# Local attention on one core: weighted values laid out by features, softmax weights divided before their transposes, q's unit length inside the exponential

## The chip, the cores and the metric

The kernel runs on one core of a Trainium2 chip. The metric is the device time of one execution in microseconds. Before the change three executions took 3894.79, 3896.19 and 3896.57 us; their median is 3896.19 us. The profile is of a further execution, which took 3893.85 us; the span of its instructions is 3892.1 us.

## The reference

The input is 8 sequences of 512 tokens with 128 features, in float32. Two blocks follow each other, each with a layer norm ahead, a layer norm behind and a residual. The first is a causal attention with a Taylor-expanded exponential. The second, which the change concerns, is a stack of six layers. Each has local attention with 16 heads of 64 features and windows of 32 tokens, and a gated feed-forward part:

```python
q = l2norm(q) * qs;  k = l2norm(k) * ksc            # unit length, then a scale by feature
q = q * cos * scale + rotate_half(q) * sin * scale  # rotary; k with 1 / scale
# a window of 32 queries sees its own 32 keys and the 32 before: bk2, bv2
sim = jnp.einsum('bhwie,bhwje->bhwij', bq, bk2) * 8.0
mask = (it < jb) | (it > jb + w) | (jb == -1)
sim = jnp.where(mask, -max, sim)
attn = jax.nn.softmax(sim, -1)
out = jnp.einsum('bhwij,bhwje->bhwie', attn, bv2)
x = x + out.reshape(b, n, INNER) @ Wo
# then x = x + (a * gelu(gate)) @ W2 + b2 of a layer norm of x
```

The length of q is one number for a token and a head. Since the rotation is linear, this number may be multiplied in before or after it, or into the scores.

## The kernel before

**Stages.** The first block is done in the first 535 us of the span. The rest is one loop over steps t. A unit is a block of 128 tokens of one sequence in one layer: 6 layers x 8 sequences x 4 blocks are 192 units. Each step begins one unit and goes on with the units begun up to six steps earlier, so that a step holds projections of unit t, scores of unit t-1, weighted values of unit t-2 and the output projection of unit t-3. After the fourth block of a sequence the feed-forward part follows in pieces, one piece a step: the norm with its four transposes (`feed_norm`), `feed_first` (transposes of the normed tokens), `feed_middle` (the hidden products and gelu), `feed_last`. So four steps make a cycle, each with another piece in it.

**What a step computes.** `proj` multiplies the tokens with the weights of q (s = 0) or k (s = 1) on PE (L421). DVE multiplies the result by the rotary tables (`turned` L429, `straight` L436), ACT squares it (L444), DVE adds the squares up (L457), POOL adds the two rotary parts (L454). `unit_length` turns the sums of squares into inverse lengths on ACT, and POOL multiplies q and k by them (L470). `by_features(c)` transposes q and k of four head pairs on PE (by the helper of L70), and ACT copies them out of PSUM (L514). `values` makes the values (L481), which ACT copies (L482) and seven DMAs on SP's queue spread over windows. `scores` writes a mask into PSUM by a product with a 128x128 unit matrix in BF16 (L527), twice, for even and odd heads; adds the products of q and k, 64 of them of 64x32 stationary and 64 moving columns (L534); takes the row maxima on DVE (L542), 16 exponentials on ACT, one a head (L546), and the sums and their reciprocals on DVE (L552, L553). `by_keys` transposes the unnormed weights (L564 copies). `weigh_values` multiplies with the weights as stationary operand (64x32) and the values as moving operand (64 columns) (L574), giving tokens by features; DVE divides by the sums (L582). `out_by_features` transposes the result (L70, copies L596), and `out_project` multiplies by Wo (L603) and adds into the state (L608).

**Order.** On PE the order is the order of the program text, fixed by hand. On the other engines a scheduler decides, with copies out of PSUM raised in priority and with a few hand-written orders (`issue_behind`). The order on PE within a step, with the unit's lag behind, is: `proj` q (0), `out_project` (3), `proj` k (0), `by_keys` (2), `values` (0), `by_features(0)` (1), `weigh_values` (2), `by_features(4)` (1), the feed-forward piece, `scores` (1), `out_by_features` (2).

**Buffers in PSUM.** The tag mm has two buffers of two banks (projections, values, hidden products), tr has two of one bank (all transposes and the output projection), and s has one of two banks, which scores and weighted values use in turn. Buffers are given out in the order of the program.

A float32 product is two passes on PE, each with its own weight load, so 64 products are 128 records of each kind.

## Time and profile before

| what | before |
|---|---|
| median of three runs | 3896.19 us |
| the profiled execution | 3893.85 us, span 3892.1 us |
| PE busy | 3729.8 us (96%), 65600 products and as many weight loads |
| DVE busy | 2818.2 us (72%) |
| ACT busy | 2657.5 us (68%) |
| POOL busy | 1837.0 us (47%) |
| mean busy share of the DMA engines, 535 to 3810 us | 26% |
| granted TensorE clock | 0.99 |

A name such as `tr<-ident,qk` means that the instruction writes the tile tr and reads ident and qk. L70 is the line of a helper that all transposes share, so transposes are told apart by their tiles. Busy PE is not PE at its peak, since products are pipelined and their ends are modelled; where the pace of PE matters, the distance between starts is used.

### The profile page before, as it was taken

What the parts mean: (1) busy time and instruction counts of PE and PEld (TensorE: products, weight loads), DVE (VectorE), ACT (ScalarE), POOL (GpSimd) and SP (SyncE); (2) the same over time, 40 slices, a digit from 0 to 9 for tenths busy, and PEclk for the clock granted to TensorE, in tenths of its full rate; (3) what the DMA queues carried; (4) which work ended last, traced back from release to release, by engine and by line L of the source; (5) the groups of instructions that cost most, each with busy time, mean ns of one, the idle gap of its engine ahead of it and who ended that gap; (6) DMA issues with size and microseconds to landing.
All of it is one profiled execution on the core that took longest, in us unless ns stands there. A gap on an engine that the chain in (4) does not pass through costs nothing.

```text
span 3892.1 us, 149565 instructions
## 1 busy us (share of the span) xinstructions
PE 3729.8 (96%) x65600; PEld 2474.2 (64%) x65600; DVE 2818.2 (72%) x4300; ACT 2657.5 (68%) x6745; POOL 1837.0 (47%) x1311
## 2 busy tenths in 40 slices
PE   8999989999999999999999999999999999999997
PEld 4555456666666666666666666666666666666665
DVE  4555567777867777777777777777787777777775
ACT  5565656776767777777777677777677777766664
POOL 0000025555555555555555555555555555555552
PEclk9999999999999999999999999999999999999998
DMA  2000012222222222222222322223222222222221
GB/s 81 17 9 12 6 50 71 59 66 60 76 74 63 63 63 66 71 75 65 60 62 64 82 65 66 65 56 82 70 66 59 66 65 56 65 68 68 64 67 37
DMA packets 153208, 233.46 MB, mean 60 GB/s; under 512 B 32622, under 2 KB 53356, under 8 KB 151788
## 3 DMA queue, kind: packets, MB, share of 16 engines
q1 hardware_dynamic: 152556, 223.89, 22.4%
q8 instruction: 517, 8.47, 0.9%
q14 instruction: 135, 1.11, 0.1%
HBM read 24.54 MB, written 4.19 MB: 7 GB/s over the span
## 4 chain that ended last, share of the span: by engine, by line
PE 89%; ACT 5%; issue 3%; DVE 2%; DMA 0%; POOL 0%; POOLq 0%; DVEq 0%; SPq 0%; ACTq 0%
PE tr L70 17%; PE mm L421 17%; PE mm L481 9%; PE py L603 9%; PE sp L534 7%; PE po L574 6%; PE y L282 4%; PE mm L625 3%; PE py L657 3%; PE mm L626 3%; PE sc L252 2%; PE sp L527 2%; ACT sq L444 2%; PE vv L230 2%; PE po L318 2%
## 5 line engine op out<-in xcount | busy, mean ns | idle before, releaser
L454 POOL TENSOR_TENSOR qk<-t,t 128x1024 f32<-128x1024 f32 x384 | 909.2, 2368 | 999.6 <-DVE t L436 999.5
L421 PE MATMUL mm<-wqkv,state 128*128 128x512 f32 x1536 | 727.1, 596 | 3.7 <-ACT v L482 2.6
L470 POOL TENSOR_TENSOR qk<-qk,ss 128x1024 f32<-128x1024 f32 x384 | 722.3, 1902 | 16.0
L429 DVE TENSOR_TENSOR t<-mm,tab 128x512 f32<-128x512 f32 x768 | 497.8, 685 | 242.8 <-PE mm L421 231.3
L546 ACT ACTIVATE pe<-sp,mx 128x64 f32<-128x64 f32 x3072 | 651.4, 376 | 27.6 <-DVE mx L542 27.3
L436 DVE TENSOR_TENSOR t<-mm,tab 128x1024 f32<-128x1024 f32 x384 | 465.9, 1213 | 0.0
L457 DVE TENSOR_REDUCE ss<-sq 128x16 f32<-128x1024 f32 x384 | 461.9, 1203 | 2.0 <-ACT sq L444 2.0
L444 ACT ACTIVATE sq<-mm 128x512 f32<-128x512 f32 x768 | 422.6, 610 | 47.2 <-DVE t L436 45.6
L603 PEld LDWEIGHTS py<-oT,wo 128*128 128x128 f32 x3072 | 374.8, 193 | 93.5 <-issue 56.2
L70 PEld LDWEIGHTS tr<-ident,qk 128*128 128x128 f32 x3072 | 345.7, 141 | 127.1 <-issue 105.7
L70 PE MATMUL tr<-ident,qk 128*128 128x128 f32 x3072 | 412.1, 277 | 7.4 <-ACT qT L514 2.3
L596 ACT COPY oT<-tr 128x512 f32<-128x512 f32 x384 | 207.3, 589 | 266.2 <-PE tr L70 265.2
L421 PEld LDWEIGHTS mm<-wqkv,state 128*128 128x128 f32 x1536 | 264.1, 192 | 191.6 <-issue 188.0
L481 PE MATMUL mm<-wqkv,state 128*128 128x512 f32 x768 | 367.9, 602 | 16.8 <-ACT sq L444 16.8
L603 PE MATMUL py<-oT,wo 128*128 128x128 f32 x3072 | 376.0, 276 | 1.0 <-ACT oT L596 0.9
L582 DVE TENSOR_TENSOR on<-po,su 128x1024 f32<-128x1024 f32 x192 | 235.1, 1224 | 170.1 <-PE po L574 170.1
L534 PEld LDWEIGHTS sp<-kT,qT 64*32 64x32 f32 x24576 | 271.9, 106 | 116.7 <-issue 113.8
L574 PE MATMUL po<-v,pT 64*32 64x64 f32 x24576 | 299.3, 225 | 44.7 <-issue 44.7
L482 ACT COPY v<-mm 128x1024 f32<-128x1024 f32 x192 | 194.5, 1013 | 211.0 <-PE mm L481 211.0
L534 PE MATMUL sp<-kT,qT 64*32 64x64 f32 x24576 | 312.2, 227 | 26.0 <-issue 25.2
L574 PEld LDWEIGHTS po<-v,pT 64*32 64x32 f32 x24576 | 258.5, 105 | 86.4 <-issue 86.2
L542 DVE TENSOR_REDUCE mx<-sp 128x16 f32<-128x1024 f32 x192 | 234.6, 1222 | 106.9 <-PE sp L534 106.3
(108 smaller groups left out, 5171.0 us busy)
## 6 DMA issues: line engine op xcount, KB each, us to landing
v<-v SPq DMA_DIRECT2D x1152, 128.0 KB
v<-v SPq DMA_DIRECT2D x672, 64.0 KB
wqkv<-in_L_ffn_Wqkv_dram SPq DMA_DIRECT2D x6, 1536.0 KB
wo<-in_L_ffn_Wo_dram SPq DMA_DIRECT2D x6, 512.0 KB
xin<-_attn_hidden_states_dram SPq DMA_DIRECT2D x8, 256.0 KB
xr<-_attn_hidden_states_dram SPq DMA_DIRECT2D x8, 256.0 KB
x<-xr SPq DMA_DIRECT2D x8, 256.0 KB
xr<-x SPq DMA_DIRECT2D x8, 256.0 KB
```

Of the source, the lines that this page charges most:

```text
L70: nc.tensor.transpose(ps[:cols, :rows], src, ident[:rows, :rows])
L421: nc.tensor.matmul(ps[:, a].rearrange("p h d -> p (h d)"), lhs, wqkv[:, s, a, :], start=True, stop=True)
L429: nc.vector.tensor_tensor(t2[:, a], ps[:, 1 - a], tab[:, 2 * s + 1, j, HF * a : HF * (a + 1)].unsqueeze(1).to_broadcast([P, H, HF]), ALU.mult,
L436: nc.vector.tensor_tensor(t1, ps, tab[:, 2 * s, j, :].rearrange("p (a d) -> p a d", a=2).unsqueeze(2) .to_broadcast([P, 2, H, HF]), ALU.mult,)
L444: nc.scalar.activation(sq[:, :, a, :], ps[:, a], AF.Square)
L454: nc.gpsimd.tensor_tensor(qk[:, s].rearrange("p h a d -> p a h d"), t1, t2, ALU.add)
L470: nc.gpsimd.tensor_tensor(t, t, ss[:, i, :].unsqueeze(2).to_broadcast([P, H, HD]), ALU.mult)
L481: nc.tensor.matmul(ps[:, p, :], lhs, L["wqkv"][:, 2, p, :], start=True, stop=True)
L534: nc.tensor.matmul(sp[W * w : W * (w + 1), p, pair, :], qT[HD * p : HD * (p + 1), pair, W * w : W * (w + 1)], kT[HD * p : HD * (p + 1), pa ...
L546: ex = nc.scalar.activation(pe[:, pair, p, :], sp[:, p, pair, :], AF.Exp, bias=mx[:, p, pair : pair + 1])
L574: nc.tensor.matmul(po[W * w : W * (w + 1), p, pair, :], pT[r, pair, W * w : W * (w + 1)], v2[r, w, HD * pair : HD * (pair + 1)], start=Tru ...
L603: nc.tensor.matmul(py, L["wo"][:, c, :], oT[:, c, :], start=(c == 0), stop=(c == NP - 1))
```

## The change

Eight edits come together.

1. `weigh_values` swaps operands: the values are stationary (64x64) and the weights move (32 columns), so that the result comes out by features. ACT copies it in one piece of 128x1024. `out_by_features` is gone, and Wo's rows are reordered on the host to fit.
2. The division by the sums moves ahead of `by_keys`: two halves, each a sum and a reciprocal on DVE and a product on POOL.
3. q is no longer multiplied by its inverse length on POOL. The 16 exponentials take it as a scale by token, and one small product on DVE applies it to the row maxima.
4. The mask product has 32 rows and a 32x128 stationary matrix (`each`), even and odd heads on different rows; the first block of a sequence keeps the 128-row form.
5. The copy of the values is split: half on ACT, half on DVE, with `values` in two halves.
6. The order on PE becomes `proj` q, `out_project`, `proj` k, `by_features(0)`, first half of `values`, `by_keys`, second half of `values`, `weigh_values`, `by_features(4)`, the feed-forward piece, `scores`.
7. New orders by hand: squares of q behind the exponentials, copies of `by_features` behind the squares of q, the rotary products of k (`turned`) behind the reciprocals, POOL's additions behind the divisions.
8. The gelu table is loaded behind the copies of `by_keys`, no longer ahead of the step.

```diff
+    each = const.tile([2 * W, P], BF16, tag="each", name="each")
...
     def gelu_only():
         ld = nc.scalar.preload_act_table_set("gelu_and_others")
-        issue_behind(ld, exps[-1])
+        issue_behind(ld, pcopies[-1])
...
-            nc.vector.tensor_tensor(
+            t = nc.vector.tensor_tensor(
                 t2[:, a], ps[:, 1 - a],
...
+            if s == 1 and sums:
+                issue_behind(t, sums[-1])
...
+            q2 = nc.scalar.activation(sq[:, :, a, :], ps[:, a], AF.Square)
+            if s == 0:
+                if exps:
+                    issue_behind(q2, exps[-1])
+                qsquares.append(q2)
...
+        add = nc.gpsimd.tensor_tensor(qk[:, s].rearrange("p h a d -> p a h d"), t1, t2, ALU.add)
+        if divisions:
+            issue_behind(add, divisions[-1])
...
-        for i in range(2):
-            t = qk[:, i].rearrange("p h a d -> p h (a d)")
...
+        t = qk[:, 1].rearrange("p h a d -> p h (a d)")
+        nc.gpsimd.tensor_tensor(t, t, ss[:, 1, :].unsqueeze(2).to_broadcast([P, H, HD]), ALU.mult)
...
+        nc.tensor.matmul(ps[:, half, :], lhs, L["wqkv"][:, 2, half, :], start=True, stop=True)
+        if half == 0:
+            nc.scalar.copy(v0[:, 0], ps[:, 0])
+            return
+        nc.vector.tensor_copy(v0[:, 1], ps[:, 1])
...
-                nc.scalar.copy(dst, ps)
+                cp = nc.scalar.copy(dst, ps)
+            issue_behind(cp, qsquares[-1])
...
         for p in range(2):
+            r = slice(W * p, W * (p + 1))
+            lhs, mk = (identb, mask0) if u["j"] == 0 else (each[r], mask[r])
             nc.tensor.matmul(
-                sp[:, p], identb, mk.unsqueeze(1).to_broadcast([P, NP, 2 * W]),
+                sp[:, p], lhs, mk.unsqueeze(1).to_broadcast([lhs.shape[0], NP, 2 * W]),
...
+        rn = u["ss"][:, 0, :].rearrange("t (c p) -> t c p", p=2)
...
             nc.vector.tensor_reduce(mx, sp, AX.X, ALU.max, negate=True)
+            nc.vector.tensor_tensor(mx, mx, rn.rearrange("t c p -> t p c"), ALU.mult)
...
-                    pe[:, pair, p, :], sp[:, p, pair, :], AF.Exp, bias=mx[:, p, pair : pair + 1]
+                    pe[:, pair, p, :], sp[:, p, pair, :], AF.Exp,
+                    bias=mx[:, p, pair : pair + 1], scale=rn[:, pair, p : p + 1],
...
-        su = f2.tile([P, NP, 2], F32, tag="su", name="su")
-        nc.vector.tensor_reduce(su, pe, AX.X, ALU.add)
-        nc.vector.reciprocal(su, su)
+        for c in range(0, NP, 4):
+            part = pe[:, c : c + 4].rearrange("t c p k -> t (c p) k")
+            su = f2.tile([P, NP], F32, tag=f"su{c}", name="su")
+            with tc.high_priority():
+                nc.vector.tensor_reduce(su, part, AX.X, ALU.add)
+                rc = nc.vector.reciprocal(su, su)
+                dv = nc.gpsimd.tensor_tensor(
+                    part, part, su.unsqueeze(2).to_broadcast([P, NP, 2 * W]), ALU.mult
+                )
...
-        po = psum.tile([P, 2, NP, HD], F32, tag="s", name="po", bufs=1)
...
+        po = psum.tile([P, 2, NP // 2, P], F32, tag="s", name="po", bufs=1)
+        for k in range(NP // 2):
             for w in range(4):
+                for i in range(2):
+                    for p in range(2):
+                        r, c, o = slice(HD * p, HD * (p + 1)), 2 * k + i, HD * (i ^ p)
+                        nc.tensor.matmul(
+                            po[o : o + HD, p, k, W * w : W * (w + 1)],
+                            v2[r, w, HD * c : HD * (c + 1)],
+                            pT[r, c, W * w : W * (w + 1)],
+                            start=True, stop=True, skip_group_check=True,
+                        )
+        u["oT"] = oT = f1.tile([P, 2, NP // 2, P], F32, tag="oT", name="oT")
         with tc.high_priority():
-            dv = nc.vector.tensor_tensor(
...
+            nc.scalar.copy(oT, po)
...
-            if gelus:
-                gelu_only()
             at(t, 0, proj, 0)
             at(t, 3, out_project)
             at(t, 0, proj, 1)
-            at(t, 2, by_keys)
...
-            at(t, 0, values)
...
+            at(t, 1, by_features, 0)
+            at(t, 0, values, 0)
+            at(t, 2, by_keys)
+            if gelus:
+                gelu_only()
+            at(t, 0, values, 1)
...
-            at(t, 1, by_features, 0)
             at(t, 2, weigh_values)
...
             at(t, 1, scores)
-            at(t, 2, out_by_features)
```

## The prediction

> **What bounds the kernel now.** I first read busy shares and the chain that ended last on the page.
>
> ```profile
> span 3892.1 us, 149565 instructions
> ...
> PE 3729.8 (96%) x65600; PEld 2474.2 (64%) x65600; DVE 2818.2 (72%) x4300; ACT 2657.5 (68%) x6745; POOL 1837.0 (47%) x1311
> ...
> PE 89%; ACT 5%; issue 3%; DVE 2%; DMA 0%; POOL 0%; POOLq 0%; DVEq 0%; SPq 0%; ACTq 0%
> ```
>
> PE is the bound, with ACT and DVE in 7% of the chain. The timeline of PE for one step (start, length, instructions) says where:
>
> ```profile
> 2067.54 1.88 PE L421 MATMUL mm<-wqkv,state 128*128 128x512 f32 x4
> 2069.26 1.95 PE L603 MATMUL py<-oT,wo 128*128 128x128 f32 x16
> 2071.05 1.88 PE L421 MATMUL mm<-wqkv,state 128*128 128x512 f32 x4
> 2072.76 1.04 PE L70 MATMUL tr<-ident,pe 128*128 128x128 f32 x8
> 2073.64 1.88 PE L481 MATMUL mm<-wqkv,state 128*128 128x512 f32 x4
> 2075.36 1.04 PE L70 MATMUL tr<-ident,qk 128*128 128x128 f32 x8
> 2076.32 1.49 PE L574 MATMUL po<-v,pT 64*32 64x64 f32 x128
> 2077.74 1.09 PE L70 MATMUL tr<-ident,qk 128*128 128x128 f32 x8
> 2078.67 0.60 PE L70 MATMUL nx<-ident,state 128*128 128x128 f32 x4
> 2079.12 0.59 PE L527 MATMUL sp<-mask,identb 128*128 128x512 bf16 x2
> 2079.65 1.61 PE L534 MATMUL sp<-kT,qT 64*32 64x64 f32 x128
> 2081.19 1.09 PE L70 MATMUL tr<-ident,on 128*128 128x128 f32 x8
> 2082.12 1.88 PE L421 MATMUL mm<-wqkv,state 128*128 128x512 f32 x4
> ```
>
> One piece starts where the last ends: 14.58 us without a wait. From the starts of q's projection between 665 and 3258 us, the four kinds of step take on average 20.2 (hidden products), 17.0 (last products), 15.1 (norm) and 15.9 (transposed norm): 68.2 us a cycle, 48 cycles. The norm lengthens DVE's work, so the step after it is late (15.9 for a like amount of PE work).
>
> What the other engines do in this step:
>
> ```profile
> 2068.26 3.39 ACT L546 ACTIVATE pe<-sp,mx 128x64 f32<-128x64 f32 x16
> ...
> 2072.04 1.09 ACT L444 ACTIVATE sq<-mm 128x512 f32<-128x512 f32 x2 [0.39 <-DVE t L436]
> ...
> 2077.84 1.23 DVE L582 TENSOR_TENSOR on<-po,su 128x1024 f32<-128x1024 f32 x1 [0.41 <-PE po L574]
> ```
>
> The exponentials follow each other every 0.196 us ((3.39 - 0.45)/15) and end 4.1 us after the step's start; their transposes run at 5.2. That slack of 1.1 us is what the change draws on.
>
> **The skill.** "ScalarE: Activation LUTs", What ACT_TABLE_LOAD costs: each operand read by a [128,1] pointer adds about 93 ns to an activation. The trace agrees for one pointer: groups by shape have `ln_rs<-ln_mv,eps` (4 elements, pointer bias) at 297 ns but `ss<-ss` (32 elements, none) at 230, and gelu on 128x512 (pointer) at 687 against 610 for the square. No run here shows two pointers. "TensorE: Matmul & The Clock Gate", LDWEIGHTS: a load takes its columns / 1.2 ns, whatever its rows. The timeline agrees: `vs<-cb,tw`, 128 weight columns and 4 moving, starts 16 times between 15.47 and 17.35 us, 0.117 each. "TensorEngine Tiling (Array Packing)", Key Properties: tiles load and multiply independently. Eight passes of L282 (128x64 weights, 512 moving) start at 27.82 and the next piece at 29.69: 1.87, where L421 needs 1.72 for four, so two column tiles do run side by side.
>
> **What PE gains, by part.**
>
> - `out_by_features` goes: 0.93 us (2081.19 to 2082.12).
> - Mask: two products over 0.53. On different rows they can run together: minus half of the 0.43 that the chain gives them, 0.21, in three steps of four: 0.16.
> - Weighted values: now 1.42 from start to start. Each pass will load 64 columns and move 32, so loads set the pace: half of 0.117, 0.058 on a tile; four tiles side by side make 0.0147 a pass, times 128 is 1.88. I take 1.85: +0.43. Lower end 0 (if issue alone sets the pace, as the old 1.42/128 = 0.011 could be); upper end, two loads on the same rows not side by side, 128 x 0.029 = 3.7: +2.3.
>
> Sum -0.66 a step, 127 us in 192: what the change brings if PE stays the bound.
>
> **What the other engines lose.** ACT per step: two copies of oT (2 x 0.48 paced) become one of about 1.0 (as L482, 1013 ns); half of L482 leaves (-0.5); the scale pointer adds 0.085 (mean of the trace's 0.077 and the skill's 0.093) to each of 16 exponentials: +1.36. DVE: minus 1.22 (L582), plus 0.65 for half the values (L234: 687 ns), 0.25 for the product on the maxima (like L553: 243 ns), 0.25 for a second reciprocal and 0.1 for splitting the sum: even. POOL: minus 1.9 (L470), plus two products of 128x512 at 1.04 (the additions of 512 and 1024 elements in L677 and L454 give 2.15 ns an element; 1902 less 512 x 1.67 for the broadcast form): even. Eight copies for `each` (under 1 us once) and the DMAs, whose number stays, lie beside other work.
>
> No engine is full, but the chain around the softmax grows at both ends. Before, `out_by_features` gave the maxima 0.93 us of cover, so the exponentials began 0.72 after the step's start. Now scores are PE's last work: maxima 0.2 to 1.4, product to 1.65, exponentials from 1.7. A walk through a step, in us after its start, in the order in which each engine has its instructions:
>
> - ACT: exponentials issued to 1.7 + 16 x 0.281 = 6.2, done 6.3; squares of q (0.49 each) to 7.2, the first done at 6.8; copies qT, kT to 8.15, done 8.3.
> - DVE: second sum 6.4 to 7.05, reciprocal 7.3; POOL's second division 7.4 to 8.45.
> - PE, free at 6.1 after `by_features(0)`: first half of `values` waits for the square, 6.85 to 7.7; `by_keys` waits for the copy of qT, 7.95, and for the second division, 8.6 to 9.0; second half of `values` to 9.9; weighted values to 11.75; `by_features(4)` to 12.6. Without waits this would be 11.2: 1.4 lost.
> - DVE after the reciprocal: `turned`, sum of squares, `turned`, `straight` of k to 10.95. ACT: squares of k to 12.0, oT to 12.95, then qT and kT of the second half to 14.0. The mask needs the buffer of the weighted values, so it waits for oT; the second half of the scores waits for kT.
>
> Then mask 0.31 and scores 1.5. Hidden products (2042.94 to 2048.17: 5.23) cover oT: 12.6 + 5.23 + 1.81 = 19.65; last products (2.58): 17.0; to both 0.15 for the gaps called issue, which now stand at 0.3 and which waits partly fill. Norm step: mask at 13.05, kT at 14.0, end 14.9, call it 15.0. Step after it: DVE's norm now precedes the maxima whole, and ACT's squares of k come 0.7 later, so exponentials start 3.2 after the step's start (before: 1.66 in the step from 2082.12). Everything shifts by 1.5: squares of k end 13.5, oT 14.5, qT 15.0; the norm's transposes take the PSUM buffer that this copy frees: 15.0 to 15.6; mask and scores to 17.4. The old mask once a cycle adds 0.2. Sum 19.8 + 17.15 + 15.0 + 17.4 + 0.2 = 69.55, against 68.2: +1.35 a cycle, x48 = +65 us. On the profiled execution (span 3892.1, time 3893.85) that is 3957 and 3959; on the median, 2.3 us above it, 3961.
>
> Queued behind the new waits: on POOL the divisions hold back the additions (2.37 each, L454), but with these, the copy of kT and the product on k (1.9) POOL is done near 17 us, ahead of k's transposes in the next step (5.6 us into it). On SP the DMAs of the second half of the values wait for DVE's copy, which ends at 11.65; the products that read them come a whole step later, so they stay hidden. The gelu table moves behind pT: 9.7 to 11.0, where ACT waits for `straight`, so it costs nothing; if DVE were earlier, it would cost up to its 1.28 in one step of four.
>
> **Rivals.**
>
> *PE gain comes through (faster).* The scale pointer is free, or bias and scale are read together. Then exponentials end 1.36 earlier; the path through the first reciprocals and the divisions holds back 0.9 of this on the two PE-heavy steps, so each gains about 0.45; norm step -0.45, the step after -0.8: 67.4 a cycle, -38 us, 3858. With weighted values at the old pace also, 65.8: 3781. For it: PE 96% busy, 1.1 us of slack. Against: one pointer costs its time in this trace. It decides near a pace of 0.23 us for an exponential.
>
> *Weight loads on the same rows don't overlap.* Weighted values 3.7, all on PE's path: +1.85 more a step, 3961 + 355 = 4316. For it: no 64x64 tile in this trace. Against: today's 64x32 loads, 27 ns by the skill's price, start every 0.011, closer than two row halves alone would allow (0.0135).
>
> *Gain and loss cancel.* The walk leans on waits of a few tenths; within 0.2% (8 us, about what a measurement here can tell from no change) is a narrow slot.
>
> **Numbers.** Slower through the longer softmax chain 0.54; loads not overlapping 0.07; PE gain through 0.34; cancel 0.05. So slower 0.61, same 0.05, faster 0.34. Likeliest time 3961; its own range, from 0.2 us less to 0.3 more a step, 3915 to 4025. The range over all leaves out half of the rival with old pace and the loads: 3810 to 4040.
>
> **What would show it.** Right: exponentials every 0.28 us; PE waiting before `values` on squares and before `by_keys` on POOL or ACT, 1 to 1.5 us a step; weighted values 1.8 from start to start; no L70 on `on`; the step after the norm over 17 us. Wrong: exponentials still every 0.2 us, PE without waits, weighted values near 1.4 or 3.7.

## The result, and the profile after

The changed kernel took 4364.5 us (4356.4 to 4366.3) where the kernel before took 3895.5 (3892.3 to 3896.6): the ratio is 1.120, with a 95% interval of 1.118 to 1.122. The forecast was 3961 us. The side was right; of the 469 us that it became slower, 65 were foreseen.

The page of the changed kernel, the busy shares and the chain that ended last:

```profile
PE 3832.1 (88%) x64064; PEld 2472.2 (57%) x64064; DVE 2905.0 (67%) x4884; ACT 2834.1 (65%) x6558; POOL 1879.6 (43%) x1503
...
PE 57%; ACT 25%; DVE 12%; issue 5%; ACTq 0%; POOL 0%; DMA 0%; DVEq 0%; POOLq 0%; SPq 0%
ACT pe L567 18%; PE mm L493 10%; PE tr L77 9%; PE po L606 9%; PE sp L552 5%; DVE mx L562 5%; ACT sq L454 4%; PE y L289 3%; PE mm L643 3%; PE py L675 3%; PE mm L644 3%; DVE mx L563 2%; PE sc L259 2%; PE mm L428 2%; PE vv L237 1%
```

PE's share of the chain fell from 89% to 57%, and the exponentials (L567) alone hold 18%. PE alone is no longer the bound: the chain now runs through the softmax on ACT and DVE, and PE waits for it inside nearly every step. Here is PE's timeline of a norm step of the changed kernel (start, length, instructions), the counterpart of the step that the prediction showed:

```profile
2260.33 1.98 PE L428 MATMUL mm<-wqkv,state 128*128 128x512 f32 x4
2262.15 1.95 PE L621 MATMUL py<-oT,wo 128*128 128x128 f32 x16
2263.93 1.88 PE L428 MATMUL mm<-wqkv,state 128*128 128x512 f32 x4
2265.65 1.07 PE L77 MATMUL tr<-ident,qk 128*128 128x128 f32 x8
2268.06 1.12 PE L493 MATMUL mm<-wqkv,state 128*128 128x512 f32 x2 [1.33 <-ACT sq L454]
2269.02 1.04 PE L77 MATMUL tr<-ident,pe 128*128 128x128 f32 x8
2269.89 1.09 PE L493 MATMUL mm<-wqkv,state 128*128 128x512 f32 x2
2270.91 2.07 PE L606 MATMUL po<-pT,v 64*64 64x32 f32 x128
2272.91 1.09 PE L77 MATMUL tr<-ident,qk 128*128 128x128 f32 x8
2273.84 0.60 PE L77 MATMUL nx<-ident,state 128*128 128x128 f32 x4
2274.38 0.39 PE L545 MATMUL sp<-mask,each 32*128 32x512 bf16 x2
2274.69 1.71 PE L552 MATMUL sp<-kT,qT 64*32 64x64 f32 x128
2276.33 1.98 PE L428 MATMUL mm<-wqkv,state 128*128 128x512 f32 x4
```

It lasts 16.0 us against 14.58. The transposes of `on` (0.93) are gone and the mask takes 0.31, as announced; weighted values take 2.00 from start to start instead of 1.42, and 1.33 us are a wait of `values` for the squares of q. ACT in the same step shows what those squares stand behind:

```profile
2262.18 4.85 ACT L567 ACTIVATE pe<-sp,mx,ss 128x64 f32<-128x64 f32 x16 [4.87 <-DVE mx L563]
2266.82 1.18 ACT L454 ACTIVATE sq<-mm 128x512 f32<-128x512 f32 x2
```

Sixteen exponentials follow each other every 0.29 us ((4.85 - 0.49)/15 = 0.291; the median distance of two starts in the whole run is 0.290), where it was 0.196. The list of waits of the changed kernel (engine, waiting piece, releaser; us in total, times, longest), from which two of the six longest are shown, says that PE's wait for the squares is the rule: the weight load of `values` has it in 189 of 192 steps, with 1.65 us each (312.0 over 189).

```profile
ACT pe L567 <- DVE mx L563: 648.0, 189, 5.5
...
PEld mm L493 <- ACT sq L454: 312.0, 189, 4.1
```

By kinds of step, as the prediction counted them (average distances between the starts of q's projection in the middle of the run, in us; the forecast of a cycle holds 0.2 more for the old mask):

| | hidden products | last products | norm | after the norm | cycle |
|---|---|---|---|---|---|
| before | 20.2 | 17.0 | 15.1 | 15.9 | 68.2 |
| forecast | 19.8 | 17.15 | 15.0 | 17.4 | 69.55 |
| after | 21.1 | 21.4 | 16.6 | 18.8 | 77.9 |

48 times the 8.36 us that the cycle is longer than forecast are 401 us, nearly all that was missed. Half of it is in one kind, the step with the last products. There the small product on the row maxima does something that it does in no other step; the timelines of VectorE and POOL:

```profile
2239.15 1.23 DVE L562 TENSOR_REDUCE mx<-sp 128x16 f32<-128x1024 f32 x1 [0.27 <-PE sp L552]
2240.48 1.88 DVE L563 TENSOR_TENSOR mx<-mx,ss 128x16 f32<-128x16 f32 x1
...
2261.91 0.17 DVE L563 TENSOR_TENSOR mx<-mx,ss 128x16 f32<-128x16 f32 x1
```

```profile
2240.05 0.29 POOL L481 TENSOR_SCALAR ss<-ss 128x32 f32<-128x32 f32 x1 [6.87 <-issue]
2240.43 1.90 POOL L483 TENSOR_TENSOR qk<-qk,ss 128x1024 f32<-128x1024 f32 x1
```

The same product of 16 elements takes 0.17 us in the next step, and 1.88 here, where it starts 0.05 us behind POOL's product on k and ends 0.03 behind it. 47 of the 192 take longer than 0.3 us (median 1.88); the median of the others is 0.176.

### The profile page after: what moved, and what is told of

It is laid out like the page before. It is cut to its first block, busy times and chain, and to the rows that moved or that the text cites. A ratio compares the mean times of both kernels' runs of the same rounds, so it can differ in the third digit from the quotient of the medians.

```text
span 4354.7 us, 148166 instructions
## 1 busy us (share of the span) xinstructions
PE 3832.1 (88%) x64064; PEld 2472.2 (57%) x64064; DVE 2905.0 (67%) x4884; ACT 2834.1 (65%) x6558; POOL 1879.6 (43%) x1503
## 3 DMA queue, kind: packets, MB, share of 16 engines
q1 hardware_dynamic: 152556, 223.89, 19.6%
## 4 chain that ended last, share of the span: by engine, by line
PE 57%; ACT 25%; DVE 12%; issue 5%; ACTq 0%; POOL 0%; DMA 0%; DVEq 0%; POOLq 0%; SPq 0%
ACT pe L567 18%; PE mm L493 10%; PE tr L77 9%; PE po L606 9%; PE sp L552 5%; DVE mx L562 5%; ACT sq L454 4%; PE y L289 3%; PE mm L643 3%; PE py L675 3%; PE mm L644 3%; DVE mx L563 2%; PE sc L259 2%; PE mm L428 2%; PE vv L237 1%
## 5 line engine op out<-in xcount | busy, mean ns | idle before, releaser
L567 ACT ACTIVATE pe<-sp,mx,ss 128x64 f32<-128x64 f32 x3072 | 931.3, 441 | 657.8 <-DVE mx L563 648.0
L579 POOL TENSOR_TENSOR pe<-pe,su 128x512 f32<-128x512 f32 x384 | 400.8, 1044 | 1187.2 <-DVE su L578 1027.4
L428 PE MATMUL mm<-wqkv,state 128*128 128x512 f32 x1536 | 748.1, 610 | 2.5 <-issue 1.9
L493 PE MATMUL mm<-wqkv,state 128*128 128x512 f32 x768 | 475.7, 704 | 269.1 <-ACT sq L454 266.5
L606 PEld LDWEIGHTS po<-pT,v 64*64 64x64 f32 x24576 | 391.0, 136 | 222.3 <-ACT pT L594 143.7
L77 PE MATMUL tr<-ident,qk 128*128 128x128 f32 x3072 | 434.5, 279 | 81.8 <-DVE state L626 73.4
L606 PE MATMUL po<-pT,v 64*64 64x32 f32 x24576 | 418.9, 221 | 61.6 <-issue 61.5
L577 DVE TENSOR_REDUCE su<-pe 128x8 f32<-128x512 f32 x384 | 261.5, 681 | 194.1 <-ACT pe L567 187.6
L428 PEld LDWEIGHTS mm<-wqkv,state 128*128 128x128 f32 x1536 | 263.7, 191 | 211.3 <-issue 192.2
L483 POOL TENSOR_TENSOR qk<-qk,ss 128x1024 f32<-128x1024 f32 x192 | 365.3, 1903 | 16.0
L614 ACT COPY oT<-po 128x1024 f32<-128x1024 f32 x192 | 195.1, 1016 | 196.8 <-PE po L606 196.8
L493 PEld LDWEIGHTS mm<-wqkv,state 128*128 128x128 f32 x768 | 128.0, 209 | 321.3 <-ACT sq L454 312.0
```

Of the source, the lines that this page charges most:

```text
L77: nc.tensor.transpose(ps[:cols, :rows], src, ident[:rows, :rows])
L428: nc.tensor.matmul(ps[:, a].rearrange("p h d -> p (h d)"), lhs, wqkv[:, s, a, :], start=True, stop=True)
L493: nc.tensor.matmul(ps[:, half, :], lhs, L["wqkv"][:, 2, half, :], start=True, stop=True)
L567: ex = nc.scalar.activation(pe[:, pair, p, :], sp[:, p, pair, :], AF.Exp, bias=mx[:, p, pair : pair + 1], scale=rn[:, pair, p : p + 1],)
L606: nc.tensor.matmul(po[o : o + HD, p, k, W * w : W * (w + 1)], v2[r, w, HD * c : HD * (c + 1)], pT[r, c, W * w : W * (w + 1)], start=True, ...
```

## The experiments

Expected of each run is what was written before it ran. "After" below is the changed kernel, and edits have the numbers of the change: 1 weighted values by features, 2 division on POOL, 3 q's unit length as scale, 4 the mask; the rest (5 to 8) is called the new order. Each kernel is compared with runs of the kernel before on the same chip; where this document puts kernels side by side in us, it is the ratio times 3895.5. Code cuts leave out lines at "...", and declarations of tiles.

### Taking parts away from the changed kernel

**The scale pointer.** The exponentials read no scale, and the maxima are multiplied by a tile of ones, so that all instructions stay but the second pointer goes. q's unit length is left out with it.

```
-            nc.vector.tensor_tensor(mx, mx, rn.rearrange("t c p -> t p c"), ALU.mult)
+            nc.vector.tensor_tensor(mx, mx, ones, ALU.mult)
...
-                    bias=mx[:, p, pair : pair + 1], scale=rn[:, pair, p : p + 1],
+                    bias=mx[:, p, pair : pair + 1],
```

> The kernel after, with the exponentials' scale operand left out and the small product on the row maxima done with a tile of ones in place of q's inverse length. It leaves out q's unit length, so each exponential has one pointer operand; all else stays, the two-input product on DVE too. Chain theory (16 exponentials with a second pointer, 0.29 in place of 0.20 us each, stand in the chain of every step): minus 1.5 us in most of 192 steps, 150 to 280 us, so 4085 to 4215. Port theory (the loss comes from DVE's small product waiting for POOL): the exponentials speed up but the time stays above 4320.

4090.3 us, ratio to before 1.051 (1.049 to 1.053): 270 us less than the changed kernel. The exponentials are back at 0.197. But the run took away two things: the product on the maxima no longer needs `ss`, starts ahead of POOL's product on k (in 46 steps by less than 0.03 us), and took 0.177 us on average, 0.40 at most. The granted clock rose too, from 0.966 to 0.991 (of which more below). So the 270 us are not the price of the pointer alone. And 198 us of loss remain without it. PE's waits in this run have moved from the squares to the division:

```profile
PEld tr L81 <- POOL pe L582: 246.7, 383, 3.8
```

**POOL's product on k in four pieces** of 128x256: the same work and dependencies, shorter instructions.

```
-        nc.gpsimd.tensor_tensor(t, t, ss[:, 1, :].unsqueeze(2).to_broadcast([P, H, HD]), ALU.mult)
+        for h in range(0, H, 4):
+            nc.gpsimd.tensor_tensor(
+                t[:, h : h + 4], t[:, h : h + 4],
+                ss[:, 1, h : h + 4].unsqueeze(2).to_broadcast([P, 4, HD]), ALU.mult,
+            )
```

> The kernel after, with POOL's product of k by its inverse length in four pieces of 128x256 in place of one of 128x1024. Port theory (DVE's product on the row maxima, which reads two SBUF tiles, stands still until the POOL instruction of 1.90 us ends, in one step of four): the small product takes at most 0.6 us in place of 1.88, 48 steps gain 1.3 to 1.7 us, so 4280 to 4305. Rival (the 1.88 us are a wait for data, or are hidden): no change, 4355 to 4375.

4244.4 us, 1.091 (1.088 to 1.093): 115 us less, more than the 60 to 85 expected, though POOL's work became longer. The product's group by shape (count, busy us, mean ns) in the changed kernel:

```profile
L563 DVE TENSOR_TENSOR mx<-mx,ss 128x16 f32<-128x16 f32 x192 | 111.9, 583 | 20.5 <-DVE mx L562 1.4
```

and in this run:

```profile
L567 DVE TENSOR_TENSOR mx<-mx,ss 128x16 f32<-128x16 f32 x192 | 53.4, 278 | 20.5 <-DVE mx L566 1.4
L484 POOL TENSOR_TENSOR qk<-qk,ss 128x256 f32<-128x256 f32 x768 | 446.8, 614 | 16.0
```

In 48 steps the product now takes 0.59 us, one POOL piece, where it took 1.88, one whole POOL product. So VectorE stands still for as long as the POOL instruction lasts that it met: shown. (Not every POOL instruction does it: in the run with edit 3 alone 35 of these products ran beside a memset on POOL, which reads no tile, and took 0.18 us at most.) The gain, 115 us, is nearly twice the 48 x 1.29 us of the product itself; the other half came from the clock (below).

**Edit 3 undone**: POOL multiplies q and k again, no scale, no product on the maxima.

```
+        for i in range(2):
+            t = qk[:, i].rearrange("p h a d -> p h (a d)")
...
-            nc.vector.tensor_tensor(mx, mx, rn.rearrange("t c p -> t p c"), ALU.mult)
...
-                    bias=mx[:, p, pair : pair + 1], scale=rn[:, pair, p : p + 1],
+                    bias=mx[:, p, pair : pair + 1],
```

> The kernel after without edit 3: POOL multiplies q and k by their inverse lengths as before, the exponentials have one pointer and the product on the maxima is gone. Chain and port theories together: the gain of the first two experiments and 0.25 us more, 230 to 380 us, so 3985 to 4135. If the weight loads of the 64x64 products and the order on PE make the loss: above 4250.

4092.4 us, 1.051 (1.050 to 1.053), as expected, and the same as without the pointer. (VectorE's order differs here, as told under edit 2 below.)

**Edit 1 undone**: weighted values by tokens, a plain copy, `out_by_features` back at the end.

```
-                            po[o : o + HD, p, k, W * w : W * (w + 1)],
-                            v2[r, w, HD * c : HD * (c + 1)],
-                            pT[r, c, W * w : W * (w + 1)],
+                        po[W * w : W * (w + 1), p, pair, :],
+                        pT[r, pair, W * w : W * (w + 1)],
+                        v2[r, w, HD * pair : HD * (pair + 1)],
...
+            at(t, 2, out_by_features)
```

> The kernel after without edit 1: weights stationary (64x32), result by tokens, copied by DVE without a division, transposed and copied by ACT as before, behind the scores. Chain theory: the transposes cost PE 0.93 us a step but cover the row maxima, so they are free; weighted values gain 0.58 (2.00 to 1.42): 4364 minus 80 to 150, so 4215 to 4285. If PE is still the bound: plus 0.93 minus 0.58 in 192 steps, 4430. Load theory (the swap is most of the loss): below 4100.

4362.8 us, 1.120 (1.118 to 1.122): no change, and all three expectations missed. PE's transposes of `on` come back, and weighted values go from 2.44 to 1.90 us on average. But the run is no price of edit 1. In every step counted the first sum and its reciprocal now stand ahead of `straight` of q on VectorE, where in the changed kernel they stand behind it:

```profile
2257.56 0.20 DVE L578 RECIPROCAL su<-su 128x8 f32<-128x8 f32 x1
2257.80 1.22 DVE L446 TENSOR_TENSOR t<-mm,tab 128x1024 f32<-128x1024 f32 x1
```

In the norm step the exponentials end 1.0 us earlier than in the changed kernel (5.63 against 6.64), but the squares behind them only 0.5 (7.15 against 7.62), since they wait for `straight`.

**Squares of q between the exponentials**: eight exponentials, both squares, eight exponentials (`weights(u, 4)`, the pairs 4 to 7); sums and division follow the second eight, and the copies of `values` and of the transposed weights are fixed behind all sixteen.

```
+                if c0 and qsquares:
+                    issue_behind(ex, qsquares[-1])
...
             at(t, 0, proj, 0)
+            at(t, 2, weights, 4)
```

> The changed kernel with the squares of q between the first and the last eight exponentials instead of behind all sixteen. Theory that the wait of the first half of values for the squares is what sets the end of a step: 0.8 to 1.2 us a step come back, 4130 to 4210 us. Rival, that the exponentials with the second sum, reciprocal and division behind them are a second chain of the same length, so that by_keys only waits in its place: 4330 to 4430 us.

4882.5 us, 1.253 (1.250 to 1.256). Now `values` starts 6.2 us after the start of a norm step instead of 7.7, but the last exponential ends at 9.0 instead of 6.6, and PE waits before `by_keys`:

```profile
PEld tr L77 <- POOL pe L598: 829.8, 384, 4.5
```

The direction is the rival's: behind the exponentials hangs a second chain (second sum, reciprocal, division, transposes), as long as the one through the squares. The loss was larger than the rival said: copies of q and k came between the exponentials too, and the mean granted clock fell to 0.911.

### Doing parts alone, in the kernel before

**Mask alone** (edit 4).

```
-        mk = mask0 if u["j"] == 0 else mask
...
+            r = slice(W * p, W * (p + 1))
+            lhs, mk = (identb, mask0) if u["j"] == 0 else (each[r], mask[r])
```

> The kernel before with edit 4 alone (mask of 32 rows in three steps of four). Theory that PE is the bound of the kernel before: the 0.15 us a step by which the mask product shortened in the changed kernel (0.53 to 0.38 on average) comes through whole, 29 us: 3860 to 3872 us. Rival, that waits around the scores absorb it: 3885 to 3897 us.

3892.7 us, 0.998 (0.997 to 0.999): 9 us, not 29. From start to start the mask fell from 101.2 us in all to 71.7, but the scores behind it rose from 324.9 to 338.4, where PE stands still more often for no reason that the profile shows ("issue", 34.5 us instead of 25.2); the expectation that a PE at 96% passes on each gain was wrong.

**Edit 3 alone.**

```
+            nc.vector.tensor_tensor(mx, mx, rn.rearrange("t c p -> t p c"), ALU.mult)
...
-                    pe[:, pair, p, :], sp[:, p, pair, :], AF.Exp, bias=mx[:, p, pair : pair + 1]
+                    pe[:, pair, p, :], sp[:, p, pair, :], AF.Exp, bias=mx[:, p, pair : pair + 1],
+                    scale=rn[:, pair, p : p + 1],
```

> The kernel before with edit 3 alone (q's unit length as scale of the exponentials and a product on the maxima, POOL multiplies k only). Theory that the longer exponentials (0.29 us each where 0.20 were) use up the slack of 1.1 us in any order of the work: they end 5.6 instead of 4.1 us after the start of a step, 0.4 to 1.0 us a step is lost, 3970 to 4090 us, more where the product on the maxima stands still for POOL's product on k. Rival, that the old order hides them and only the new order exposes them: 3870 to 3925 us.

4346.7 us, 1.114 (1.112 to 1.117): slower than both theories, though POOL lost half of its products. From the start of `by_keys` to the next piece, `values`, it is 2.86 us a step, 1.01 before. The transposes themselves wait little; most of it is `values`, which waits for the squares of q behind the longer exponentials (300.1 us, in all 192 steps). In the norm step that wait is 0.44 us: the slack of 1.1 us that the prediction read off is used up. It is 2.7 us in the step with hidden products, and there ScalarE's order has changed as well:

```profile
2305.42 1.28 ACT L82 ACT_TABLE_LOAD   x1
2306.71 1.07 ACT L564 COPY pT<-tr 128x512 f32<-128x512 f32 x2
2307.67 1.11 ACT L444 ACTIVATE sq<-mm 128x512 f32<-128x512 f32 x2
```

The copies of the transposed weights stand ahead of the squares, where in the kernel before they stood behind them. In 46 steps, moreover, the product on the maxima takes 1.76 us, and the mean granted clock is 0.964. So the 1.114 holds more than the pointer's price.

**Edit 2 alone.**

```
+        for c in range(0, NP, 4):
+            part = pe[:, c : c + 4].rearrange("t c p k -> t (c p) k")
...
+                nc.gpsimd.tensor_tensor(
+                    part, part, su.unsqueeze(2).to_broadcast([P, NP, 2 * W]), ALU.mult
+                )
...
+            dv = nc.vector.tensor_copy(on.rearrange("t c p d -> t p c d"), po)
```

> The kernel before with edit 2 alone (weights divided on POOL in two halves ahead of their transposes, a plain copy out of the weighted values). Theory that sum, reciprocal and division (0.65, 0.25 and 1.04 us) behind the exponentials outlast the slack of 1.1 us: by_keys waits 0.6 to 1.2 us a step, 4000 to 4120 us. Rival, that POOL's queue decides, where a division stands behind a product of 1.9 or an addition of 2.4 us: over 4200 us. Rival, that it is hidden: 3880 to 3910 us.

4887.4 us, 1.253 (1.251 to 1.255): over 4200, the range of the rival about POOL's queue, but not for its reason. In 189 steps POOL stands idle until the reciprocals come (584.7 us in all), so it is not its queue that holds the divisions. Timelines of PE and of ACT in one step of this run:

```profile
2306.39 0.66 PE L70 MATMUL tr<-ident,pe 128*128 128x128 f32 x4 [1.05 <-POOL pe L557]
2307.39 0.66 PE L70 MATMUL tr<-ident,pe 128*128 128x128 f32 x4 [0.34 <-POOL pe L557]
2309.71 3.48 PE L481 MATMUL mm<-wqkv,state 128*128 128x512 f32 x4 [1.67 <-ACT sq L444]
```

```profile
2308.08 0.59 ACT L570 COPY pT<-tr 128x512 f32<-128x512 f32 x1 [0.41 <-PE tr L70]
2308.56 2.08 ACT L444 ACTIVATE sq<-mm 128x512 f32<-128x512 f32 x4
```

`values` waits behind `by_keys`, which waits for POOL, and then runs at half speed (3.48 for 1.88). It is held twice, for here too ScalarE has the squares behind the copies of the transposed weights, in every step, and these copies wait for `by_keys`. The mean granted clock is 0.909. On VectorE the sums stand ahead of `straight`; with this same order there, edit 2 costs 393 us in the new order (below) and 986 here. So the new order, with transposes and half of `values` ahead of `by_keys` and with the squares fixed behind the exponentials, keeps the division from costing this much; which part of it does was not tested.

**Mask and table.** Two parts together: the mask, and the gelu table behind the copies of `pT` instead of behind the exponentials.

```
-        issue_behind(ld, exps[-1])
+        issue_behind(ld, pcopies[-1])
```

> The kernel before with two parts of the change: the mask of 32 rows and the gelu table loaded behind the copies of the transposed weights instead of behind the exponentials. Theory that the table's 1.28 us stand on the path in one step of four: 0.6 to 1.0 us a cycle beyond the mask's gain, 3840 to 3865 us. Rival, that the table was hidden: as with the mask alone, 3885 to 3898 us.

3871.5 us, 0.9925 (0.9911 to 0.9940): faster than both kernels, by less than expected. The step with hidden products takes 19.6 instead of 20.2: the squares of q and the copies of the transposed weights no longer stand behind the table, and `values` starts 6.17 us after the step's start instead of 6.62. PE is busy for 96% of the span and holds 91% of the chain.

### Building the change up, from the order

**Order and mask** (edits 1, 2, 3 undone). Against the kernel before, this remains of PE's order:

```
-            at(t, 2, by_keys)
...
-            at(t, 0, values)
+            at(t, 1, by_features, 0)
+            at(t, 0, values, 0)
+            at(t, 2, by_keys)
...
+            at(t, 0, values, 1)
```

> The changed kernel with edits 1, 2 and 3 undone: what is left is the new order on PE (by_features of q ahead of values, values in two halves around by_keys, out_by_features gone back to the end), the gelu table behind the copies of the weights, the other hand orders, and the mask of 32 rows. Theory that the order costs by itself, since values now waits for both squares behind the exponentials: 3930 to 4010 us. Rival, that the order is harmless while the exponentials are short: the mask's gain remains, 3855 to 3895 us.

3967.1 us, 1.017 (1.015 to 1.018). The order costs by itself, but not through the squares, for which PE hardly waits here. In the norm step the mask waits for VectorE's division of the weighted values (L607), which ends at 2114.4, behind `turned`, `straight`, the copy of half of the values and a sum of squares, and `turned` of k behind the reciprocal (2108.2 to 2114.4 without a longer gap than 0.6). PE's timeline of this run:

```profile
2114.42 0.39 PE L548 MATMUL sp<-mask,each 32*128 32x512 bf16 x2 [1.66 <-DVE on L607]
```

The norm step takes 16.5 (15.1 before), the next 17.2 (15.9), and the hidden one 19.3 (20.2), where the table is out of the way.

**Edit 3 on top of it** (edits 1 and 2 undone).

```
+        su = f2.tile([P, NP, 2], F32, tag="su", name="su")
+        nc.vector.tensor_reduce(su, pe, AX.X, ALU.add)
+        rc = nc.vector.reciprocal(su, su)
```

> The changed kernel with edits 1 and 2 undone: new order and mask (3967 us) plus edit 3, with sum and division where the kernel before has them. Theory that the pointer of the scale and the product on the maxima that stands still for POOL cost the same 270 us whatever follows: 4210 to 4260 us. Rival, that they cost so much only because two divisions on POOL hang behind the exponentials: 4020 to 4130 us.

4230.2 us, 1.084 (1.082 to 1.086): 262 us more than order and mask, as expected. Divisions behind the exponentials are not needed for the pointer and the product on the maxima to cost this much.

**Edit 2 on top of it** (edits 1 and 3 undone, as in the runs above with one of them undone).

> The changed kernel with edits 1 and 3 undone: new order and mask (3967 us) plus edit 2. Theory that the divisions cost 125 us in the new order, and edit 1 nothing: 4075 to 4110 us. Rival, that edit 1 costs part of the 125 (its weighted values take 2.00 us where 1.42 were) and the divisions less: 3985 to 4060 us.

4358.4 us, 1.118 (1.115 to 1.121): as slow as the whole change, and neither theory foresaw it. VectorE's timeline of this run shows why (two lines of ACT after it):

```profile
2254.24 0.69 DVE L578 TENSOR_REDUCE su<-pe 128x8 f32<-128x512 f32 x1
2254.85 0.32 DVE L579 RECIPROCAL su<-su 128x8 f32<-128x8 f32 x2
2255.20 1.22 DVE L446 TENSOR_TENSOR t<-mm,tab 128x1024 f32<-128x1024 f32 x1
```

```profile
2250.62 3.39 ACT L568 ACTIVATE pe<-sp,mx 128x64 f32<-128x64 f32 x16
2256.51 1.08 ACT L454 ACTIVATE sq<-mm 128x512 f32<-128x512 f32 x2 [2.50 <-DVE t L446]
```

Sums and reciprocals stand ahead of `straight` of q here, the squares wait for `straight` (2.5 us behind the last exponential), and `values` for the squares. The scheduler orders VectorE anew for each variant; in the changed kernel `straight` comes first. So this run does not price the division, and neither do the runs with edit 3 and with edit 1 undone price theirs, where one sum stands ahead of `straight` (in most steps and in all).

**The same two, with the changed kernel's order on VectorE**: a hand order puts the sums behind `straight`, and in the program's text the sums and the addition of q's rotary parts move behind q's projection.

```
+                if straights:
+                    issue_behind(r0, straights[-1])
```

Edit 2 on top of order and mask:

> As order, mask and division (edits 1 and 3 undone, 4358 us), with one thing more: the sums of the softmax stand behind the product `straight` of q on VectorE, as they do in the changed kernel. Theory that the 391 us of edit 2 there came from VectorE's order (sums and reciprocals ahead of `straight`, for which the squares wait, for which values waits): squares of q end near 5.1 us after a step's start instead of 7.3, values starts near 6.2 instead of 7.8, and only by_keys' wait for the second division is left, 0.5 to 0.9 us a step over the order with the mask: 4060 to 4140 us. Rival, that the divisions themselves hold PE: 4300 to 4380 us.

4154.2 us, 1.067 (1.065 to 1.069). The 393 us of edit 2 shrink to 195: half of them were VectorE's order. The time is just above what the theory gave (4060 to 4140): `values` starts at 6.75, not 6.2, since the second group of transposes waits for the PSUM tile that the addition to `state` reads, and that addition stands between the sums:

```profile
PEld tr L77 <- POOL pe L593: 245.7, 384, 3.0
...
PE tr L77 <- DVE state L648: 83.5, 190, 0.8
```

Edits 1 and 2 on top of order and mask:

> As the changed kernel with edit 3 undone (4092 us), with the sums of the softmax behind the product `straight` of q on VectorE. Theory that VectorE's order holds values back there too (7.2 us after a step's start): values starts near 6.2, by_keys' second half then waits for the second division at 8.2 to 8.4 instead of 8.6: 4030 to 4070 us. Rival, that the chain through the divisions is just as long: 4080 to 4110 us.

4079.9 us, 1.047 (1.045 to 1.050), between the two, at the rival's lower edge. `values` starts at 6.8, but the second half of `by_keys` at 8.7, where it was 8.6 without the hand order; the division sets it.

With `straight` ahead of the sums on VectorE in all of them, the ladder reads, in parts of the time before: order and mask +1.7% (65 us), division +5.0% (195), weighted values by features -2.0% (76), scale and product on the maxima +7.3% (284). Of the last step, k's product in pieces gave back 115 us, so some 170 are left for the longer exponentials; that is an estimate, since no run took away the pointer alone. And the same ladder inside a norm step, in us after its start (means of 33 to 38 steps of each run):

| | before | order, mask | + division | + edit 1 | after |
|---|---|---|---|---|---|
| first exponential | 0.72 | 0.72 | 0.72 | 1.50 | 1.79 |
| last exponential ends | 4.11 | 4.12 | 4.12 | 4.89 | 6.64 |
| second square of q ends | 5.59 | 5.59 | 5.60 | 5.87 | 7.62 |
| first half of `values` | 6.10 | 6.10 | 6.75 | 6.82 | 7.67 |
| `by_keys`, second half | 5.66 | 7.39 | 8.62 | 8.69 | 9.08 |
| weighted values | 8.78 | 8.85 | 10.06 | 10.14 | 10.53 |

(Before, `by_keys` came first.) The last column shows the two chains: exponentials, squares, `values`; and exponentials, sum, division, `by_keys`. Without the pointer (first run above) the last exponential ends 1.5 us earlier, but weighted values start only 0.4 earlier (10.15), because the second chain is close behind the first.

## Why the prediction was wrong

The mechanism that the prediction bet on, a longer softmax chain that holds PE, is the one that came. Its size failed, by three steps: in the walk through a step `values` was let go by the first square of q, and it waits for the second; the product on the maxima was put at 0.25 us without asking what POOL does at that time, and takes 1.88 in one step of four; and a wait was priced at its length alone, while the clock of PE falls behind two of them. Weighted values were also put in too low.

**The bound, and PE's gain.** PE with its one piece after another was the bound before, right. The gain was right for `out_by_features` (0.93 gone) and for the mask (0.53 to 0.38: 0.15, forecast 0.16). Weighted values failed: 1.85 was put in, "loads set the pace" with four tiles side by side. The median is 2.00, and the mean from start to start went from 1.73 to 2.44, since in 60 of the 192 steps (62 before) PE also stands still inside the piece, for no reason that the profile shows:

```profile
2287.86 1.48 PE L606 MATMUL po<-pT,v 64*64 64x32 f32 x86
2290.20 0.83 PE L606 MATMUL po<-pT,v 64*64 64x32 f32 x42 [0.86 <-issue]
```

The prediction priced the change between two undisturbed steps. It is +0.59 a step over the forecast: 0.15 of pace and 0.44 of standing still, whose cause stays open. The loads do overlap: the rival with 3.7 is excluded.

**The softmax chain, the step that failed most often.** Forecast and measured in a norm step: exponentials from 1.7 (1.79), the last ends 6.3 (6.64), first square of q done 6.8 (7.13), `values` 6.85 (7.67), `by_keys` 7.95 and 8.6 (8.63 and 9.08), second half of `values` 9.0 (9.52), weighted values 9.9 (10.53). Two terms: the second pointer adds 0.094 an exponential, not 0.085, and the last one takes 0.49; and `values` was let go by the first square. It waits for the second, 0.49 later, because q's projection is one PSUM tile of two halves, given back as a whole: in all 384 pairs of squares of the trace only the second one carries the signal. So halving `values` could not let it start at the first square; whether a tile in two parts would, no run here shows. With 0.63 at weighted values and 0.59 inside them, 1.22 us a step or 234 us in 192 steps.

**The product on the maxima, 0.25.** The step named a row of like size, which reads one tile where the product reads two, and did not ask what POOL does at that time. Where POOL is not at work the product takes 0.176, better than forecast; in the step after hidden products, where the unit lengths come late behind gelu's table, it meets POOL's product on k and takes 1.88. 1.63 x 47 = 77 us. The Trainium skill has it ("SBUF — State Buffer", section "SBUF: two separate sides"): of a VectorE instruction with two SBUF inputs and a GpSimd instruction that reads SBUF, the one that starts first gets the shared ports for the whole instruction, and "the other fully blocks". The trace agrees: 1.88 beside 1.90, 0.59 beside 0.61 with the product in pieces, and 0.177 on average without the pointer, where VectorE starts first in 46 steps. The prediction did not look there.

**What followed from the waits.** Nothing in the prediction priced a wait at more than its length. In the stretch after the blocked product PE has two waits close together (1.16 and 1.57 us), and what comes next runs at half speed. PE's timeline, and then busy times of each engine with PE's granted clock (third figure from the end) in two stretches, both of the changed kernel:

```profile
2248.33 1.19 PE L493 MATMUL mm<-wqkv,state 128*128 128x512 f32 x2 [1.57 <-ACT sq L454]
2249.31 1.91 PE L77 MATMUL tr<-ident,pe 128*128 128x128 f32 x8
2251.02 1.85 PE L493 MATMUL mm<-wqkv,state 128*128 128x512 f32 x2
```

```profile
2244.00:2249.30 5.30, 2.57 (x12) 1.29 (x11) 3.97 (x9) 5.24 (x16) 1.65 (x2) 1.00 0.00 0
2249.30:2252.80 3.50, 3.50 (x12) 2.05 (x10) 2.54 (x3) 2.69 (x5) 3.50 (x3) 0.52 0.01 2
```

The Trainium skill ("TensorE: Matmul & The Clock Gate", Part 1) says that the array's clock falls to half after an idle window of about 3.4 us and comes back after as long a busy one. This case needs less than an idle window: the longest wait here is 1.57 us, PE was at work for 2.57 of 5.30 us, and still the next 3.5 us had a clock of 0.52. The trace's record of the granted clock shows the same for the whole loop. It knows two values, full and half, and 55 of its 69 stretches at half last 3.41 us. In the 3.41 us before each of the 60 that begin in the loop PE was busy for 0.11 to 0.55 of the time (median 0.39). Of the 961 spans of that length that stayed at the full clock, none followed one in which PE was busy for less than 0.47. So the half clock went with a PE that was busy for less than about half of such a span.

In the middle of the run it is 2.87 us from `values` to weighted values in the steps with hidden products, 4.03 in those with last products, 3.49 in those after the norm: 1.16 + 0.62 = 1.78 a cycle, 85 us in 48. PE does not wait in these stretches (its idle time there is 0.01 us or less on average). Over the whole run, in the steps with last products, they take 2.86 us where the clock stayed full (12 of 46 steps) and 4.58 where it was at half (34); after the norm 2.86 (29) and 4.50 (17). So these 85 us are the clock, not more waiting. The mean clock says the same: 0.990 before, 0.966 after, 0.981 with the k product in pieces. In that last run the stretch takes 2.86 us in all 46 steps with last products, which gives back about 58 us, and about 12 come in the steps after the norm. With the 62 of the product itself this makes 132, where 115 were gained; what was lost against it elsewhere was not followed up.

234 + 77 + 85 = 396 of the 403 us between forecast and result. That the sum comes so close is in part luck, for by kinds of step it fits less well: the norm step is 1.6 us over its forecast where these terms give 1.2, and the step after it 1.4 where they give 1.8.

**What was right.** The pace of the exponentials (0.281 forecast, 0.290 measured), the pointer's price from the Trainium skill ("ScalarE: Activation LUTs", What ACT_TABLE_LOAD costs: 93 ns; 94 here, so that the mean with the trace's own 77 was the worse choice), where PE would wait (before `values` for squares in all but a few steps), POOL's division (1.04 forecast, 1.044 measured), and the table behind `pT`, which shows no cost and, in the kernel before, gains. The step after the norm is over 17 us (18.8), but partly by luck: its exponentials start 2.5 us after the step's start, not 3.2, and the time goes into the chain and the clock. PE's waits for POOL were forecast but are small after (14.8 us for the loads, against 312 for the squares): the first chain hid them.

**The rivals.** "PE gain comes through" was to be decided at a pace of 0.23; measured was 0.290. But it was wrong in a second way: without the pointer the kernel takes 4090 us, not 3858. Its own brake, the path through reciprocals and divisions, holds back more than the 0.9 us given to it: in a norm step the second half of `by_keys` starts at 8.7 and the addition to `state` delays the transposes ahead of `values`. So the chance of 0.34 for it was too large on this ground too. The range ended at 4040: it let single terms be off, but not several in one direction, and here the pace and the tail of the exponentials, the second square and the weighted values all were, which without slack add up.

## What to carry to other kernels

Where an engine is busy at 96% and another has one microsecond of slack per step, count first what the change adds to the chain that uses this slack, and then what it takes off the busy engine: here some 0.4 us a step off PE (0.93 and 0.15 less, 0.71 more) bought nothing. Of a wait, ask which tile is given back and by which of its readers; of a small VectorE instruction with two inputs in SBUF, what POOL is doing then; and of PE's waits, whether two of them stand close enough for the clock to fall. An edit measured in a variant has a price only if the order on the other engines is the same: here the scheduler moved the sums on VectorE or the squares on ScalarE in five of the variants (edits 1 and 3 undone, edit 2 on top of order and mask, edits 2 and 3 alone). So look at the order on every engine, and fix it by hand before comparing.

## What the hardware did unexpectedly

- A VectorE product of 16 elements with both inputs in SBUF took 1.88 us instead of 0.176 beside a POOL product of 1.90, and 0.59 beside POOL pieces of 0.61.
- A second pointer operand (scale beside bias) lengthened the pace of exponentials on 128x64 from 0.196 to 0.290 us.
- Weights of 64x64 with 32 moving columns ran 128 passes in 2.00 us (15.6 ns a pass); weights of 64x32 with 64 moving in 1.42 (11.1 ns).
- After 5.30 us with PE half idle, and no wait longer than 1.57 us in it, the granted clock was 0.52 for 3.5 us; in the run with edit 2 alone the mean clock fell to 0.909.
